# A fused Mamba, attention and mixture-of-experts kernel: the in-projection on 128 rows of taps, and one transfer of B and C for each chunk

## The chip, the cores and the metric

The kernel runs on one core of a Trainium2 chip, as one launch. The metric is the device time of the launch in microseconds (us); the time before is 5182.59 us, the median of three runs (5178.62 to 5191.08). The engines are called as in the profile: PE is TensorE's matmuls and PEld its weight loads, DVE is VectorE, ACT is ScalarE, POOL is GpSimd, and SP is SyncE, which here issues nearly all DMA transfers.

## The reference, cut to what matters

There are two layers on four images of 128 channels and 64x64 points (4096 tokens). The first normalises, runs a depthwise 3x3 convolution and a Mamba block, and projects; the second is attention with four heads over 4096 tokens and a mixture of eight experts. The change lies in the Mamba block. It cuts the 128 channels into four chunks of 32 that share their weights:

```python
xz = u @ in_proj_w.T                       # u: tokens x 32, in_proj_w: 128 x 32
xin, z = jnp.split(xz, 2, axis=-1)         # 64 channels each
xin = jnp.pad(xin, ((0, 0), (0, 0), (3, 0)))
xin = lax.conv_general_dilated(xin, conv1d_w[:, None, :], (1,), 'VALID', feature_group_count=di)
xin = silu(xin + conv1d_b[None, :, None])  # a causal convolution of four taps for each channel
x_dbl = xin @ x_proj_w.T
dt, Bm, Cm = jnp.split(x_dbl, [R, R + N], axis=-1)     # N = 16 states, R = 2
delta = softplus(dt @ dt_proj_w.T + dt_proj_b)
h = exp(delta * A) * h + delta * Bm * xin              # for each token, channel and state
y = einsum('bdn,bn->bd', h, Cm)
out = (y + D_skip * xin) * silu(z) @ out_proj_w.T
```

The in-projection of the first half and the convolution are both linear, so they can be one matmul: every output is a sum over 32 channels and 4 taps, 128 products in all.

## The kernel before

**Tiling.** The tokens of an image are cut into eight blocks of 512, so there are 32 blocks (b, i). Two chunks fill the 128 partitions (64 channels of each), so each block has two passes, p = 0 and 1. A pass has sixteen states, taken two at a time: a unit (b, i, p, n). There are 512 units.

**Slots.** The main loop runs over slots, two to a unit, so 1024 slots and 32 to a block; after them the loop goes on until the rest of the attention is done. Every engine works in the order in which its instructions are written. One slot writes, in this order:

1. transfers put off by `send` (they go out at the next slot's `flush`), then `fetch`: the rows of B or C of a later unit, one DMA on SP;
2. `prepared`: on ACT the decay exp(delta A) of the next unit (`da`), 128x512;
3. in even slots `driven` on DVE (h = B times du);
4. the X lane's second half-stage;
5. one group of attention: four matmuls of scores (`sc`) on PE and two exponentials of 128x1024 on ACT (`pT`);
6. in even slots `scan` on DVE, in odd slots `read` on DVE (C times h);
7. the Y lane's first half-stage;
8. `turned_on`: PE adds up and turns the terms of y;
9. the Y lane's second half-stage;
10. `weighted`: eight matmuls of the weighted sums (`av`) of the group of the slot before;
11. the X lane's first half-stage.

The scores have two PSUM buffers, so the scores of a slot wait until the exponentials of the slot before have been read out of them.

**Lanes.** Everything else runs as generators in two lanes, one stage for each half-slot (a `yield` ends a stage). A lane takes its tasks in order, and a task starts only when what it depends on is done. The Y lane holds `first_norm` (10 stages, 5 slots), `conv` (26 stages, 13 slots) and `inputs` (6 stages, 3 slots) of every block, and `group_norm` for every image. The X lane holds `closed` (18 stages, 9 slots; out-projection, projection, keys, queries and values of a block) and, from slot 2 of a block, `finished` (30 stages, 15 slots; a block's attention output and experts). Each lane has one PSUM bank, `work("X")` and `work("Y")`.

For block k the loop at L1311 appends to the Y lane: `inputs(k, 1)`, which waits for the scan of (k-1, 1); `first_norm` of block k+2; `conv` of k+1; `inputs(k+1, 0)`, which waits for the scan of (k, 0). `fetch` forces an `inputs` that isn't done by the time a unit's rows are wanted.

**The in-projection.** `conv` ends with `xn`, the normalised block with three tokens of the block before ahead of it. Four transfers of 64 partitions make `pairs`: rows 0 to 63 the two chunks of a pass, rows 64 to 127 the same one token later. `inputs` multiplies it in two accumulating matmuls (L667), a 128x128 weight for the taps 0 and 1 and one for 2 and 3. In its first stage it issues these and the matmul of z; in the second, one half-slot on, ACT's Silu of `xin` and of `zs`; in the third the matmuls `pb` (B and C) and `wdt`; in the fourth ACT's copy of B and C and the softplus in five pieces; in the sixth five DVE operations. A channel d of chunk c sits on partition 2d + c. `fetched` (L714) is one transfer of a row of B or C for both chunks to 128 partitions, 512 KB.

Of the kernel before, what the change touches and what calls it, by code (L numbers as in the profile page):

```python
# [17 lines left out]
P = 128  # L18
# [5 lines left out]
DI = 64  # L24
# [12 lines left out]
def conv_mamba_attn_moe_kernel(ctx: ExitStack, tc: tile.TileContext, t: dict):  # L37
# [37 lines left out]

    late = nc.scalar
    gmat, fc1w = (load(k, eng=late) for k in ("gmat", "fc1w"))
    inx, xdt, dtT, alog = (load(k, pool=scratch, eng=late) for k in ("inx", "xdt", "dtT", "alog"))
    cw = load("cw", [P, 4, P], t["cw"].partition_broadcast(P), pool=scratch, eng=late)
    lnw, lnb, fc1b, lcw, lcb = (load(k, eng=late) for k in ("lnw", "lnb", "fc1b", "lcw", "lcb"))  # L80
    fc2T, fc2b, cb, dtb, dsk = (load(k, eng=late) for k in ("fc2T", "fc2b", "cb", "dtb", "dsk"))
    inz, wbc, wout, projT = (load(k, eng=late) for k in ("inz", "wbc", "wout", "projT"))
# [10 lines left out]
        nc.vector.tensor_scalar_mul(taps[:, k, :], ident, fc1w[:, k : k + 1])  # L93


    inxc = const.tile([P, 2, P], F32, name="inxc")
    for j in range(4):
        r = slice(DI * (j % 2), DI * (j % 2) + DI)
        nc.vector.tensor_mul(inxc[r, j // 2, :], inx[r, :], cw[r, j, :])

    amat = const.tile([P, NST], F32, name="amat")
    nc.scalar.activation(amat, alog, AF.Exp)
# [319 lines left out]
    def send(out, in_, slots=1):  # L422
        outgoing.append([slots, out, in_])
# [24 lines left out]
    def work(lane, shape=None):  # L448
        return ps_work.tile(shape or [P, BLK], F32, tag=f"work{lane}", name=f"ps_{lane}")
# [51 lines left out]


    held = set()
    group_of, y0_of, xn_of, pairs_of, in_of, gated, kqv = {}, {}, {}, {}, {}, {}, {}
    IMAGE = "p (r w) -> p r w"
    group_of[0] = gm0, gr0

# [75 lines left out]
    def conv(b, i):  # L583
        cm = tmp("Y", "cm")
        h = work("Y") if b == 0 else cm
        half = b == i == 0

        def tap(k):
            y0 = y0_rows(b, i, k // 3, k % 3)
            w = fc1w[:, k : k + 1]  # L590

            hr = (cm if half and k > 4 else h).rearrange(IMAGE, w=IMG)
            if b == 0 and not (half and k > 4):
                mm(hr, taps[:, k, :], y0, k == 0, k == (4 if half else 8))
            elif k == 0 or half and k == 5:
                vector.tensor_scalar(hr, y0, w, fc1b, ALU.mult, ALU.add)
            else:
                vector.scalar_tensor_tensor(hr, y0, w, hr, ALU.mult, ALU.add)

        for k in range(0, 5 if half else 9, 2):  # L600
            if b:
                yield
            tap(k)
            if k < (4 if half else 8):
                tap(k + 1)
            if half and k < 4:
                tap(k + 5)
                tap(k + 6)
            if b == 0:
                yield  # L610
                if half and k == 4:
                    vector.tensor_add(cm, h, cm)
                elif k == 8:
                    scalar.activation(cm, h, AF.Identity, bias=fc1b)
            yield
        ps = transposed("Y", by_tile(cm))
        yield
        xt = yield from normalised("Y", by_tile(ps))
        ps = transposed("Y", xt)
        yield  # L620
        g = tmp("Y", "g")
        scalar.activation(g, ps, AF.Gelu, bias=lcb, scale=lcw)
        yield
        ps = work("Y")
        mm(ps, fc2T, g)
        yield
        cm = tmp("Y", "cm")
        vector.scalar_tensor_tensor(
            cm.rearrange(IMAGE, w=IMG), ps.rearrange(IMAGE, w=IMG), fc2b, y0_rows(b, i),
            ALU.add, ALU.add,  # L630
        )
        yield
        ps = transposed("Y", by_tile(cm))
        yield
        xt = yield from normalised("Y", by_tile(ps))
        ps = transposed("Y", xt)
        yield

        xn = mix.tile([P, 3 + BLK], F32, name="xn", bufs=3)
        scalar.activation(xn[:, 3:], ps, AF.Identity, bias=lnb, scale=lnw)  # L640
        if i == 0:
            gpsimd.memset(xn[:, 0:3], 0.0)
        else:
            gpsimd.tensor_copy(xn[:, 0:3], xn_of[b, i - 1][:, BLK : BLK + 3])
        xn_of[b, i] = xn

        pairs = mix.tile([P, 2, 2 + BLK], F32, name="pairs")
        for p in range(2):
            for late in range(2):
                send(  # L650
                    pairs[DI * late : DI * late + DI, p, :],
                    xn[DI * p : DI * p + DI, late : late + 2 + BLK],
                )
        pairs_of[b, i] = pairs
        yield
        yield
        yield

    def inputs(b, i, p):

        xn, pairs = xn_of[b, i], pairs_of[b, i]
        while held:
            yield
            yield
        held.add("in")
        ps = work("Y")
        summed(ps, [(inxc[:, j, :], pairs[:, p, 2 * j : 2 * j + BLK]) for j in range(2)])  # L667
        pz = work("X")
        mm(pz, inz[:, p, :], xn[:, 3:])
        yield  # L670
        xin = mix.tile([P, BLK], F32, name="xin", bufs=2)
        scalar.activation(xin, ps, AF.Silu, bias=cb)
        zs = mix.tile([P, BLK], F32, name="zs", bufs=4)
        scalar.activation(zs, pz, AF.Silu)
        yield

        pb = work("X")
        mm(pb, wbc, xin)
        ps = work("Y")
        mm(ps, wdt, xin)  # L680
        yield
        held.clear()
        bc = tmp("Y", "bc")[0:DI, :]
        scalar.copy(bc, pb[0:DI, :])
        bcd = dram.tile([2, NST // 2, 2, 2 * BLK], F32, name="bcd", bufs=4)
        send(bcd.rearrange("c n k (m q) -> (c n k m) q", m=2), bc)

        e = tmp("Y", "e")
        scalar.activation(e, ps, AF.Abs, bias=dtb)
        scalar.activation(e, e, AF.Exp, scale=-1.0)  # L690
        ln = tmp("Y", "ln")
        scalar.activation(ln, e, AF.Ln, bias=1.0)
        delta = mix.tile([P, BLK], F32, name="delta", bufs=2)
        scalar.activation(delta, ps, AF.Relu, bias=dtb)
        yield
        yield

        du = mix.tile([P, BLK], F32, name="du", bufs=2)
        lost = du
        vector.tensor_scalar(lost, e, 1.0, -1.0, ALU.add, ALU.add)  # L700
        vector.tensor_sub(lost, e, lost)
        vector.tensor_add(ln, ln, lost)
        vector.tensor_add(delta, delta, ln)
        vector.tensor_mul(du, delta, xin)
        in_of[b, i, p] = xin, zs, delta, du, bcd
        done.add(("in", b, i, p))
        yield
# [6 lines left out]
    def fetched(unit, k):  # L714

        b, i, p, n = unit
        w = mix.tile([P, 2, BLK], F32, name="rows", bufs=4)
        sync.dma_start(
            out=w.rearrange("p m q -> p (m q)"),
            in_=in_of[b, i, p][4][:, n // 2, k, :][None].to_broadcast([DI, 2, 2 * BLK]),  # L720
        )
        return w

    def decayed(unit, da, k):
# [584 lines left out]

    X.append((("y0", *blocks[1]), first_norm(*blocks[1], "X"), [("y0", *blocks[0])]))  # L1310
    for k in range(-2, len(blocks)):  # L1311
        if 0 <= k:
            b, i = blocks[k]
            Y.append((("in", b, i, 1), inputs(b, i, 1), [("scan", *blocks[k - 1], 1)] if k else []))
        if k + 2 < len(blocks):
            b, i = blocks[k + 2]
            if k + 2 == 0 or i > 0:
                upper(k + 2)
        if 0 <= k + 1 < len(blocks):
            b, i = blocks[k + 1]  # L1320
            below = [("y0", b, i + 1)] if i < NB - 1 else []
            Y.append((("xn", b, i), conv(b, i), before(k + 1, 3) + below))
            Y.append((
                ("in", b, i, 0), inputs(b, i, 0),
                before(k + 1, 2) + ([("scan", *blocks[k], 0)] if k >= 0 else []),
            ))

        if 0 < k + 2 < len(blocks) and blocks[k + 2][1] == 0:
            upper(k + 2)
# [113 lines left out]
def _laid_out(i):  # L1443
# [10 lines left out]


    def twice(a):
        return np.repeat(a, 2, axis=0)

    z = np.zeros((P, P), np.float32)
    inx, inz = z.copy(), np.zeros((P, 2, P), np.float32)  # L1460
    wout = np.zeros((P, 2, P), np.float32)
    wbc = np.zeros((P, 4, NST // 2, 2, 2), np.float32)
    xdt, dtT = np.zeros((4, P), np.float32), np.zeros((4, P), np.float32)
    for c in range(2):
        d = slice(c, P, 2)
        for p in range(2):
            s = slice(64 * p + 32 * c, 64 * p + 32 * c + 32)
            inx[s, d] = c0["in_proj_w"][:DI].T
            inz[s, p, d] = c0["in_proj_w"][DI:].T
            wout[d, p, s] = c0["out_proj_w"].T  # L1470

        wbc[d, c] = c0["x_proj_w"][2:].reshape(2, NST // 2, 2, DI).transpose(3, 1, 0, 2)
        xdt[2 * c : 2 * c + 2, d] = c0["x_proj_w"][:2]
        dtT[2 * c : 2 * c + 2, d] = c0["dt_proj_w"].T
# [5 lines left out]
    for h in range(NH):  # L1480
# [12 lines left out]
        "lcw": col(c0["lc_ln_w"]), "lcb": col(c0["lc_ln_b"]),  # L1493
        "fc1w": c0["lc_fc1_w"].reshape(C, 9), "fc1b": col(c0["lc_fc1_b"]),
        "fc2T": c0["lc_fc2_w"].T, "fc2b": col(c0["lc_fc2_b"]),
        "inx": inx, "inz": inz,
        "cw": twice(c0["conv1d_w"]).T,
        "cb": col(twice(c0["conv1d_b"])),
        "xdt": xdt, "dtT": dtT, "dtb": col(twice(c0["dt_proj_b"])),
        "wbc": wbc.reshape(P, -1), "alog": twice(c0["A_log"]),  # L1500
# [28 lines left out]
```

## Time and profile before

| | |
|---|---|
| median of three runs | 5182.59 us (5178.62 to 5191.08) |
| profiled execution, its own time | 5183.13 us |
| its span | 5180.9 us |
| mean granted TensorE clock | 0.957 |
| start, 0 to 130 us | PE busy 62.55 us |
| first image, 130 to 650 us | PE busy 356.25 of 520 us, DVE 424.94 us, clock 0.79 |
| 2600 to 3250 us | PE busy 621.57 of 650 us, DVE 535.46 us, ACT 517.93 us, clock 0.99 |
| after the last unit, 4570 to 5181 us | PE busy 567.52 of 611 us, DVE 171.89 us, ACT 303.99 us |
| matmuls of the in-projection | first at 62.0 us, last at 4459.1 us, 64 groups of four instructions |
| transfers issued | rows of B and C 1024, `pairs` 128, keys 320, values 320, queries 161 |

Busy time of an engine is the time in which at least one of its instructions runs; idle time is told with what ended it. A float32 matmul stands in the trace as two instructions. The table by stretches shows that the slots fall into three parts: a start and a first image in which attention has little to do yet, a long middle, and a tail that is attention and experts alone.

### The profile page before, as it was taken

The numbers are of one execution on the slowest core, as the hardware profiler recorded it, in microseconds if no ns is written. First come the engines' busy times: TensorE is split into PE (matmuls) and PEld (weight loads), VectorE is DVE, ScalarE is ACT, GpSimd is POOL, SyncE is SP. The second block draws the span as 40 slices with busy tenths as digits, with TensorE's granted clock in tenths as the row PEclk, the third lists the DMA queues.
The fourth block names the chain that finished last, engine by engine and source line by source line (L and its number), as shares of the span: only waits on it lengthen the run. The fifth ranks groups of instructions, "written<-read, shape, count | busy, mean of one in ns | idle before, by whom it ended". The sixth has DMA issues, their size and how long they took to land.

```text
span 5180.9 us, 62597 instructions
## 1 busy us (share of the span) xinstructions
PE 4710.1 (91%) x20684; PEld 2321.9 (45%) x20684; DVE 3835.8 (74%) x5780; ACT 3745.7 (72%) x5700; POOL 423.1 (8%) x483
## 2 busy tenths in 40 slices
PE   4567898999999998899999999999999999999997
PEld 2334444444444444444444444444444444443443
DVE  6987767877778887878788887888788877751332
ACT  4556777787787787688888787788777787656543
POOL 1111111100000000101000000000000001000000
PEclk7778999999999999899999999999999999999998
DMA  3556667677666766767766766777766666754542
GB/s 127 183 186 212 205 212 253 233 239 243 229 224 225 239 227 234 242 230 258 252 228 227 238 229 231 258 231 255 265 227 233 221 230 221 262 179 156 184 134 72
DMA packets 451693, 1131.70 MB, mean 218 GB/s; under 512 B 51858, under 2 KB 135331, under 8 KB 451363
## 3 DMA queue, kind: packets, MB, share of 16 engines
q1 hardware_dynamic: 447296, 1125.96, 64.3%
q8 instruction: 166, 2.72, 0.2%
q10 hardware_dynamic: 4066, 1.67, 0.1%
q14 instruction: 165, 1.34, 0.1%
HBM read 967.22 MB, written 143.39 MB: 214 GB/s over the span
## 4 chain that ended last, share of the span: by engine, by line
PE 59%; DVE 19%; ACT 10%; DMA 6%; issue 4%; POOL 2%; SPq 1%; DVEq 0%; ACTq 0%; POOLq 0%
PE av L406 25%; PE sc L406 14%; PE ps_X L406 9%; DVE h L406 6%; PE ps_Y L406 6%; PE y L406 5%; ACT pT L406 3%; ACT L406 2%; DVE hc L406 2%; DMA ks<-kd 2%; ACT xt L406 1%; DVE stX L406 1%; DVE du L406 1%; DMA rows<-bcd 1%; DVE cm L406 1%
## 5 line engine op out<-in xcount | busy, mean ns | idle before, releaser
L406 ACT ACTIVATE pT<-sc 128x1024 f32<-128x1024 f32 x2048 | 1984.3, 1022 | 934.3 <-PE sc L406 932.8
L406 PE MATMUL av<-pT,v 128*64 128x512 f32 x8192 | 2002.8, 610 | 10.8 <-DVE avs L406 10.8
L406 PE MATMUL sc<-qs,ks 128*128 128x512 f32 x4096 | 1302.7, 437 | 75.9 <-ACT pT L406 39.4
L406 DVE TENSOR_TENSOR_SCAN h<-da,state,h 128x1025 f32<-128x1025 f32 x512 | 1204.5, 2353 | 96.6 <-ACT h L406 62.8
L406 PEld LDWEIGHTS sc<-qs,ks 128*128 128x128 f32 x4096 | 703.1, 190 | 812.7 <-ACT pT L406 273.2
L406 PEld LDWEIGHTS av<-pT,v 128*64 128x64 f32 x8192 | 500.4, 137 | 845.7 <-issue 816.7
L406 ACT ACTIVATE da<-delta,amat 128x512 f32<-128x512 f32 x1024 | 742.9, 730 | 1.9
L406 PE MATMUL y<-ident,hc 128*128 128x128 f32 x4096 | 626.2, 284 | 64.6 <-DVE hc L406 64.6
L406 DVE TENSOR_TENSOR hc<-rows,h 128x1024 f32<-128x1024 f32 x512 | 624.6, 1220 | 15.3 <-PE y L406 5.4
L406 DVE TENSOR_TENSOR h<-rows,du 128x1024 f32<-128x1024 f32 x512 | 623.9, 1218 | 13.0 <-DMA rows<-bcd 8.5
L406 PEld LDWEIGHTS y<-ident,hc 128*128 128x128 f32 x4096 | 524.2, 147 | 229.0 <-issue 80.8
L406 ACT ACT_TABLE_LOAD x319 | 409.3, 1283 | 19.5 <-DVE zs L406 14.3
L406 POOL TENSOR_TENSOR rsX<-rsX,mhalf 128x4 f32<-128x4 f32 x92 | 203.7, 2214 | 2504.4 <-DVE rsX L406 2420.4
L406 POOL TENSOR_TENSOR rsY<-rsY,mhalf 128x4 f32<-128x4 f32 x100 | 130.7, 1307 | 2072.5 <-DVE shiftY L406 1561.5
L406 DVE TENSOR_TENSOR avs<-av,prev 128x512 f32<-128x512 f32 x96 | 66.2, 689 | 256.7 <-PE av L406 235.0
L406 PE MATMUL ps_X<-share,w_ew 128*128 128x512 f32 x432 | 213.9, 617 | 9.1 <-DVE share L406 8.8
L406 ACT ACTIVATE xt<-ps_Y,shiftY,rsY 128x128 f32<-128x128 f32 x380 | 143.6, 468 | 81.7 <-POOL shiftY L406 73.8
L406 DVE TENSOR_TENSOR share<-share,xf 128x1024 f32<-128x1024 f32 x128 | 156.0, 1219 | 16.5 <-DMA share<-sharesX 11.7
L406 ACT COPY state<-h 128x2 f32<-128x2 f32 x448 | 88.8, 198 | 92.0 <-DVE h L406 92.0
L406 DVE SCALAR_TENSOR_TENSOR cm<-y,w_fc1w,cm 128x512 f32<-128x512 f32 x195 | 145.1, 744 | 8.0 <-ACT y L406 4.5
L406 PE MATMUL ps_Y<-pairs,inxc 128*128 128x512 f32 x256 | 132.6, 643 | 15.5 <-DMA pairs<-xn 9.9
L406 PEld LDWEIGHTS ps_X<-share,w_ew 128*128 128x128 f32 x432 | 73.2, 189 | 147.0 <-issue 97.1
(248 smaller groups left out, 3437.2 us busy)
## 6 DMA issues: line engine op xcount, KB each, us to landing
rows<-bcd SPq DMA_DIRECT2D x1024, 512.0 KB
ks<-kd SPq DMA_DIRECT2D x192, 512.0 KB
qs<-qd SPq DMA_DIRECT2D x161, 512.0 KB
share<-sharesX SPq DMA_DIRECT2D x108, 512.0 KB
v<-vd SPq DMA_DIRECT2D x192, 256.0 KB
ks<-kd SPq DMA_DIRECT2D x128, 256.0 KB
avd<-avs SPq DMA_DIRECT2D x96, 256.0 KB
prev<-avd SPq DMA_DIRECT2D x96, 256.0 KB
```

What stands on the lines that cost most here:

```text
L406: return lambda *args, **kw: queued(op(*args, **kw))
```

## The change

The taps of one chunk, 32 channels times 4, now fill the 128 rows of a tile `fours`, so that one matmul of 128 rows and 64 columns makes the 64 channels of a chunk; two of them, for the two chunks, write partitions 0 to 63 and 64 to 127 of one PSUM bank. The transfers of `fours` come in two pairs: for p = 0 at the end of `conv`, for p = 1 in the fourth stage of `inputs(k, 0)`. `inputs` has eight stages (four slots) in place of six: an empty one, the in-projection just ahead of the weighted sums, then Silu of `xin` and the matmul of z, then Silu of `zs`, and the rest as before. A channel d of chunk c now sits on partition 64c + d, and `fetched` is two transfers of 64 partitions, one for each chunk. In the loop that fills the Y lane, `first_norm` of block k+2 comes ahead of `inputs(k, 1)`.

```diff
-    inx, xdt, dtT, alog = (load(k, pool=scratch, eng=late) for k in ("inx", "xdt", "dtT", "alog"))
-    cw = load("cw", [P, 4, P], t["cw"].partition_broadcast(P), pool=scratch, eng=late)
+    inx, cw, xdt, dtT, alog = (
+        load(k, pool=scratch, eng=late) for k in ("inx", "cw", "xdt", "dtT", "alog")
+    )
...
-    inxc = const.tile([P, 2, P], F32, name="inxc")
-    for j in range(4):
-        r = slice(DI * (j % 2), DI * (j % 2) + DI)
-        nc.vector.tensor_mul(inxc[r, j // 2, :], inx[r, :], cw[r, j, :])
+    inxc = const.tile([P, DI], F32, name="inxc")
+    nc.vector.tensor_mul(inxc, inx, cw)
...
-        pairs = mix.tile([P, 2, 2 + BLK], F32, name="pairs")
-        for p in range(2):
-            for late in range(2):
-                send(
-                    pairs[DI * late : DI * late + DI, p, :],
-                    xn[DI * p : DI * p + DI, late : late + 2 + BLK],
-                )
-        pairs_of[b, i] = pairs
-        yield
-        yield
-        yield
+        windows(b, i, 0)
+        yield
+        yield
+        yield
+
+    def windows(b, i, p):
+        fours = mix.tile([P, 2, BLK], F32, name="fours")
+        for c in range(2):
+            r = slice(DI * p + DI // 2 * c, DI * p + DI // 2 * (c + 1))
+            src = xn_of[b, i][r, :]
+            src = bass.AP(src.tensor, src.offset, (src.ap[0], (1, 4), (1, BLK)))
+            send(fours[:, c, :], src)
+        fours_of[b, i, p] = fours
 
     def inputs(b, i, p):
 
-        xn, pairs = xn_of[b, i], pairs_of[b, i]
+        xn, fours = xn_of[b, i], fours_of.pop((b, i, p))
         while held:
             yield
             yield
         held.add("in")
+        yield
         ps = work("Y")
-        summed(ps, [(inxc[:, j, :], pairs[:, p, 2 * j : 2 * j + BLK]) for j in range(2)])
+        for c in range(2):
+            mm(ps[DI * c : DI * c + DI, :], inxc, fours[:, c, :])
+        yield
+        xin = mix.tile([P, BLK], F32, name="xin", bufs=2)
+        scalar.activation(xin, ps, AF.Silu, bias=cb)
         pz = work("X")
         mm(pz, inz[:, p, :], xn[:, 3:])
         yield
-        xin = mix.tile([P, BLK], F32, name="xin", bufs=2)
-        scalar.activation(xin, ps, AF.Silu, bias=cb)
         zs = mix.tile([P, BLK], F32, name="zs", bufs=4)
         scalar.activation(zs, pz, AF.Silu)
+        if p == 0:
+            windows(b, i, 1)
         yield
...
-        sync.dma_start(
-            out=w.rearrange("p m q -> p (m q)"),
-            in_=in_of[b, i, p][4][:, n // 2, k, :][None].to_broadcast([DI, 2, 2 * BLK]),
-        )
+        for c in range(2):
+            sync.dma_start(
+                out=w[DI * c : DI * c + DI].rearrange("p m q -> p (m q)"),
+                in_=in_of[b, i, p][4][c, n // 2, k, :][None].to_broadcast([DI, 2 * BLK]),
+            )
...
     for k in range(-2, len(blocks)):
-        if 0 <= k:
-            b, i = blocks[k]
-            Y.append((("in", b, i, 1), inputs(b, i, 1), [("scan", *blocks[k - 1], 1)] if k else []))
         if k + 2 < len(blocks):
             b, i = blocks[k + 2]
             if k + 2 == 0 or i > 0:
                 upper(k + 2)
+        if 0 <= k:
+            b, i = blocks[k]
+            Y.append((("in", b, i, 1), inputs(b, i, 1), [("scan", *blocks[k - 1], 1)] if k else []))
...
-        d = slice(c, P, 2)
+        d = slice(DI * c, DI * c + DI)
```

The weights are laid out to match on the host, the same numbers in another order.

More of the change, by code (lines that the diff above doesn't have):

```diff
@@ L503, in conv_mamba_attn_moe_kernel @@
     held = set()
-    group_of, y0_of, xn_of, pairs_of, in_of, gated, kqv = {}, {}, {}, {}, {}, {}, {}
+    group_of, y0_of, xn_of, fours_of, in_of, gated, kqv = {}, {}, {}, {}, {}, {}, {}
     IMAGE = "p (r w) -> p r w"
@@ L1456, in twice @@
     def twice(a):
-        return np.repeat(a, 2, axis=0)
-    z = np.zeros((P, P), np.float32)
-    inx, inz = z.copy(), np.zeros((P, 2, P), np.float32)
+        return np.concatenate([a, a])
+    inz = np.zeros((P, 2, P), np.float32)
     wout = np.zeros((P, 2, P), np.float32)
@@ L1464, in _laid_out @@
     for c in range(2):
-        d = slice(c, P, 2)
+        d = slice(DI * c, DI * c + DI)
         for p in range(2):
             s = slice(64 * p + 32 * c, 64 * p + 32 * c + 32)
-            inx[s, d] = c0["in_proj_w"][:DI].T
             inz[s, p, d] = c0["in_proj_w"][DI:].T
@@ L1495, in _laid_out @@
         "fc2T": c0["lc_fc2_w"].T, "fc2b": col(c0["lc_fc2_b"]),
-        "inx": inx, "inz": inz,
-        "cw": twice(c0["conv1d_w"]).T,
+        "inx": np.repeat(c0["in_proj_w"][:DI].T, 4, axis=0), "inz": inz,
+        "cw": np.tile(c0["conv1d_w"].T, (DI // 2, 1)),
         "cb": col(twice(c0["conv1d_b"])),
```

## The prediction

> **What bounds the kernel now.** I read the busy times first, then the groups with shapes kept apart, the waits of PE and of SP's queue, and last the timeline around a pass's in-projection. From the page and the groups:
>
> ```profile
> PE 4710.1 (91%) x20684; PEld 2321.9 (45%) x20684; DVE 3835.8 (74%) x5780; ACT 3745.7 (72%) x5700; POOL 423.1 (8%) x483
> L406 PE MATMUL ps_Y<-pairs,inxc 128*128 128x512 f32 x256 | 132.6, 643 | 15.5 <-DMA pairs<-xn 9.9 <-ACT delta L406 5.6
> L406 PE MATMUL ps_X<-zs,w_wout 128*64 128x512 f32 x128 | 33.1, 595 | 0.0
> L406 ACT ACT_TABLE_LOAD x319 | 409.3, 1283 | 19.5 <-DVE zs L406 14.3
> ```
>
> PE is busy 91% of the span, so taking matmul time away looks like a sure gain. The second and third lines give its size: four instructions of the in-projection are one pass, four of the out-projection the same kind of pair that the change makes (two matmuls of 64 columns on two halves of the array), at half the busy time. But an average hides where PE isn't the limit. The timeline of one pass (p = 0 of block 12; start, duration, engine, operation):
>
> ```profile
> 1630.52 1.88 PE L406 MATMUL ps_Y<-pairs,inxc 128*128 128x512 f32 x4
> 1632.23 1.02 PE L406 MATMUL ps_X<-xn,w_inz 128*128 128x512 f32 x2
> 1632.26 1.28 ACT L406 ACT_TABLE_LOAD   x1
> 1633.56 0.69 ACT L406 ACTIVATE xin<-ps_Y,w_cb 128x512 f32<-128x512 f32 x1
> 1634.74 1.28 ACT L406 ACT_TABLE_LOAD   x1
> 1635.49 1.12 PE L406 MATMUL ps_X<-xa,w_wqn 128*128 128x512 f32 x2
> 1639.20 1.02 PE L406 MATMUL ps_Y<-xin,wdt 128*128 128x512 f32 x2
> 1641.63 1.28 ACT L406 ACT_TABLE_LOAD   x1
> 1644.23 1.28 ACT L406 ACT_TABLE_LOAD   x1
> 1647.21 0.73 PE L406 MATMUL sc<-qs,ks 128*128 128x512 f32 x2 [0.35 <-ACT pT L406]
> 1648.12 0.73 PE L406 MATMUL sc<-qs,ks 128*128 128x512 f32 x2 [0.18 <-ACT pT L406]
> 1651.92 1.02 ACT L406 ACTIVATE pT<-sc 128x1024 f32<-128x1024 f32 x1 [0.62 <-PE sc L406]
> ```
>
> ACT loads its table four times in one pass and is busy nearly all the time from 1630 to 1650 us; at 1647 PE already waits for it. Only after that does ACT wait for PE again. So a pass is a place where ACT is as late as PE, and what PE saves there may only lengthen its wait. SP's queue and the transfers that PE waits for:
>
> ```profile
> SPq L406 <- DVE hc L406: 1199.2, 301, 9.8
> PE sc L406 <- DMA ks<-kd: 35.4, 16, 5.1
> L406 SPq DMA_DIRECT2D rows<-bcd x1024: 512/519/2047, 71.4 to 4563.1; - x171
> ```
>
> SP spends much of its time waiting for a buffer of rows to come free, not issuing, and PE has waited for keys only 16 times.
>
> [...] The trace has the 1283 ns, but the next activation starts 1.30 us after the load (1632.26 to 1633.56), so I charge 1.29 us. [...]
>
> **The change part by part.** Sums are made against the profiled execution, 5183.1 us, 0.5 above the median.
>
> *Matmuls.* Eight instructions of the weighted sums start-to-start take 1.87 us, so four take 0.94; the old in-projection takes 1.72 start to start (1630.52 to 1632.23), 1.88 alone. PE's work falls by 0.78 to 0.94 us a pass; 64 passes, 50 to 60 us. That is the whole gain that there can be, nearly.
>
> *The fourth slot.* I follow both queues slot by slot through a block, with start-to-start times of the trace. An ordinary slot is 3.43 us of PE (scores 1.03, y 0.53, weighted sums 1.87) and 2.56 us of ACT (decay and copies 0.74, exponentials 1.82). Before, a pass adds to its first slot 2.58 us of PE (in-projection 1.72, z 0.86) and 3.92 of ACT (two loads, two Silus, 0.14 to empty), to its second 1.72 of PE (`pb`, `wdt`) and 5.6 of ACT (copy 0.46, 0.72, 0.65, load 1.29, 0.54, 0.67, load 1.29). After, the first slot has 0.94 of PE and nothing for ACT, which waits there as in any ordinary slot; the second 0.86 of PE and 3.92 of ACT; the third 1.72 and 5.6. So PE's work no longer lies beside ACT's, and the saving comes out of slots in which PE waits for ACT anyway. [...]
>
> *Where the slots come to lie.* Slots of a block count from 0. Before: `inputs` of p = 1 in 3 to 5 (its scan is done at 3), `first_norm` 6 to 10, `conv` 11 to 23, `inputs` of p = 0 in 24 to 26. After: p = 1 in 3 to 6, `conv` 7 to 19, p = 0 in 20 to 23, `first_norm` 24 to 28. The X lane doesn't move: `finished` 2 to 16, `closed` 17 to 26, whose normalisation on ACT (four activations, 1.6 us of it beyond cover) falls in slot 22. In the trace 11 slots lie between p = 0 and p = 1, and 21 back, as counted.
>
> For p = 0 slots 21 to 23 then hold PE 4.29 + 5.70 + 4.37 = 14.4 us (with `closed`'s 0.55 and 0.94) and ACT 6.5 + 9.8 + 3.1 = 19.4. ACT may be about 1 us late without harm, so PE stands 4 to 4.6 us, in slot 24. Before, slots 24 to 26 held PE 6.95 + 6.25 + 3.43 = 16.6 and ACT 6.5 + 8.2 + 2.6 = 17.3, and PE stood 0.73 (seen: 0.35 and 0.18). For p = 1 slots 3 to 8 sum to 28.7 us before and 28.6 after. Over a whole block the recurrence gives 142.6 us before (the trace has 145.7 as the mean of fourteen blocks from 2216 to 4256 us; DVE and DMA waits are left out of mine) with 1.4 us of PE standing, and 146.1 after with 6.5. So +3.5 us a block: 5.1 more standing, 1.6 less work.
>
> By blocks: 17 blocks with `closed` just there (11 to 30 but 15, 18, 23), 60 us. The three ends of an image (15, 23, 31), where `inputs` of p = 0 was at 19 and meets the same normalisation now, 3.3 each, 10. Blocks 4 to 10 and 18, where nothing of X lies beside p = 0: a bare pass gives +1.0, 8 us. The first four blocks are in DVE's part of the run; half of their 0.9 to 1.9 us a pass, and 2 us at the start, come back: 8 us gained.
>
> *DVE.* The nine taps of `conv` (0.74 us each) move from slots 11 to 15 to 7 to 11, beside the routing of `finished` in slot 9 (about 3 us of small operations) and behind the five operations of `du` (3 us, slot 6). By sums DVE ends 3.6 us late at slot 12, where PE wants the result; before, 0.9 us late at 16. At most 2.6 us in 20 blocks, 52 us; at least nothing, since PE's wait in slot 7 helps DVE, and a gain of 10 if the empty slots that `first_norm` now fills even things out. I take 10.
>
> *SP.* 1024 more issues of 0.52 us: 532 us on a queue that issues about 1500 in all. Queued behind each are keys, values and queries, wanted three slots later. The rows themselves are wanted three slots after. The 16 waits for keys grow by 0.52 each: 8 at most if nothing else waits; I take 5. `fours` doubles `pairs`' bytes (16 MB of 1132 MB), has half a slot more to land and issues as often; nothing. The matmul of z no longer has the in-projection ahead to cover the X lane's reading of the same bank: within the 5.
>
> Sum: 60 + 10 + 8 + 10 + 5 - 8 = +85; 5183 + 85 = 5268 us.
>
> **The rivals.** *PE decides everywhere* (faster, the other side): middle stretches are 95% PE (621.57 of 650 us), X's matmuls fill ACT's late slots, and the standing of PE doesn't grow. Then 64 times 0.94, less the half of ten early ones and 4 us for transfers: -52, 5131. It decides once X's matmuls beside a pass reach about 1.4 us a slot, or if `closed` lies two slots earlier than counted. Against it: the 0.35 and 0.18 us waits, and ACT without a gap. *No change*: the p = 0 loss is half as large and cancels the saving, 5183. *SP is late*: two issues in each slot delay keys or rows, every one of 320 key loads by 0.52 us where a quarter is felt, and more after waits for `hc`: 5225. Against it: 1199 us of waiting that would shrink first. *The halves don't run side by side*: the pair costs 1.88 again: 64 x 0.94 = 60 on top, 5328; the out-projection speaks against it.
>
> **How the numbers follow.** Chances: ACT's lag 0.52, PE everywhere 0.32, no change 0.06, SP 0.06, not side by side 0.04. This measurement can tell 0.3%, 15.5 us, from none. So faster 0.32, same 0.06, slower 0.62. The likeliest case's own range: 5205 (p = 0 loses half) to 5325 (DVE's 52 in full). To hold eight in ten it must reach into the faster case: 5125 to 5320.
>
> **What would show it.** Right: in-projection about 0.95 us a pass beside the weighted sums, 15 slots from p = 0 to p = 1 and 17 back, and PE waiting 3 to 5 us for `pT` two to four slots after the in-projection of p = 0, with PE's total wait for `pT` up by 60 us or more from 39.4. Wrong: those waits unchanged with 50 us less PE time and a shorter middle; a wait for keys or rows well over 35 us; or waits for `cm` growing from 3.6 us past 40, which would put DVE in ACT's place.

## The result, and the profile after

The changed kernel takes 5330.24 us, the median of six runs (5317.9 to 5343.06). The kernel before took 5186.3 us in the six runs beside it. The ratio is 1.0279, with a 95% interval of 1.0259 to 1.0299: slower by 144 us. The sign is the forecast's. The size isn't: 5330 lies above the forecast of 5268 and above the upper end of its range.

First the page of the changed kernel, from its parts on busy time, queues, the chain that ended last and groups:

```profile
PE 4713.2 (88%) x20684; PEld 2311.0 (43%) x20684; DVE 3843.3 (72%) x5777; ACT 3746.4 (70%) x5700; POOL 454.6 (9%) x483
...
q1 hardware_dynamic: 471872, 1142.74, 78.1%
...
PE 44%; DMA 18%; DVE 17%; ACT 13%; issue 5%; SPq 1%; POOL 1%; DVEq 0%; ACTq 0%; POOLq 0%
...
L405 DVE TENSOR_TENSOR h<-rows,du 128x1024 f32<-128x1024 f32 x512 | 623.4, 1218 | 48.9 <-DMA rows<-bcd 48.8
```

The same two parts of the kernel before, for queues and chain:

```profile
q1 hardware_dynamic: 447296, 1125.96, 64.3%
...
PE 59%; DVE 19%; ACT 10%; DMA 6%; issue 4%; POOL 2%; SPq 1%; DVEq 0%; ACTq 0%; POOLq 0%
```

A queue's columns are packets, megabytes, and the time that its packets took as a share of 16 engines' span. The bytes grew by 1.5%, the share from 64.3% to 78.1%. In the chain, DMA's part tripled, from 6% to 18%, and PE's fell from 59% to 44%. That is not the picture that was forecast, in which ACT takes PE's place; ACT grew by 3 points only. The last line of the first fence says where DVE met it: 48.8 us of waiting for rows of B and C, against 8.5 before.

PE does its part of the change. The group of the in-projection, shapes kept apart:

```profile
L405 PE MATMUL ps_Y<-fours,inxc 128*64 128x512 f32 x256 | 84.0, 650 | 8.8 <-DMA fours<-xn 8.5
```

It was 132.6 us. Yet PE's sum stayed (4710.1 to 4713.2), since the other matmuls, the same in number, grew, among them the weighted sums from 2002.8 to 2017.3 us and the scores from 1302.7 to 1307.1. The mean granted clock fell from 0.957 to 0.948.

What PE waits for in the changed kernel (total us, times, longest):

```profile
PE ps_Y L405 <- ACT xt L405: 122.5, 31, 8.0
PE sc L405 <- DMA ks<-kd: 71.0, 32, 6.6
PE sc L405 <- ACT pT L405: 50.3, 71, 3.5
...
PE ps_X L405 <- ACT xa L405: 45.9, 18, 5.3
```

Two of them in the kernel before, to compare:

```profile
PE ps_Y L406 <- ACT xt L406: 69.1, 21, 7.7
PE sc L406 <- ACT pT L406: 39.4, 117, 2.2
```

Two things grew. Waits ended by ACT, all lines added up, went from 148 to 274 us, most of the growth under `xt` and `xa` (0.3 before). Under `xt`, a step of the normalisations, ACT is for the most part not behind with its own work: it waits there for POOL itself, 163.2 us now and 73.8 before. Waits for keys doubled, from 35.4 to 71.0. And SP's queue, in its own view of waits:

```profile
SPq L405 <- DVE hc L405: 734.7, 255, 10.2
...
SPq L405 <- DMA rows<-bcd: 239.0, 413, 1.7
```

The wait for `hc` shrank from 1199.2, as expected of a queue with 1024 more issues. The second line is new in size: 239.0 us where SP waited for an earlier transfer of rows, 24.2 before. So it isn't only issuing that holds up the queue; transfers that are still under way do too.

### The profile page after: what moved, and what is told of

It is laid out like the page before. It is cut to its first block, busy times and chain, and to the rows that moved or that the text cites. A ratio compares the mean times of both kernels' runs of the same rounds, so it can differ in the third digit from the quotient of the medians.

```text
span 5331.4 us, 64105 instructions
## 1 busy us (share of the span) xinstructions
PE 4713.2 (88%) x20684; PEld 2311.0 (43%) x20684; DVE 3843.3 (72%) x5777; ACT 3746.4 (70%) x5700; POOL 454.6 (9%) x483
## 3 DMA queue, kind: packets, MB, share of 16 engines
q1 hardware_dynamic: 471872, 1142.74, 78.1%
## 4 chain that ended last, share of the span: by engine, by line
PE 44%; DMA 18%; DVE 17%; ACT 13%; issue 5%; SPq 1%; POOL 1%; DVEq 0%; ACTq 0%; POOLq 0%
PE av L405 19%; PE sc L405 11%; DVE h L405 7%; PE ps_X L405 7%; ACT pT L405 5%; PE ps_Y L405 4%; DMA rows<-bcd 4%; DMA ks<-kd 4%; PE y L405 4%; ACT L405 3%; DVE hc L405 2%; DVE cm L405 2%; SPq L405 1%; ACT xt L405 1%; DMA v<-vd 1%
## 5 line engine op out<-in xcount | busy, mean ns | idle before, releaser
L405 PE MATMUL av<-pT,v 128*64 128x512 f32 x8192 | 2017.3, 612 | 10.7 <-DVE avs L405 9.8
L405 PE MATMUL sc<-qs,ks 128*128 128x512 f32 x4096 | 1307.1, 440 | 123.4 <-DMA ks<-kd 71.0
L405 PEld LDWEIGHTS av<-pT,v 128*64 128x64 f32 x8192 | 511.7, 138 | 850.1 <-issue 815.3
L405 DVE TENSOR_TENSOR h<-rows,du 128x1024 f32<-128x1024 f32 x512 | 623.4, 1218 | 48.9 <-DMA rows<-bcd 48.8
L405 POOL TENSOR_TENSOR rsY<-rsY,mhalf 128x4 f32<-128x4 f32 x100 | 162.9, 1629 | 2883.5 <-DVE shiftY L405 2344.9
L405 ACT ACTIVATE xt<-ps_Y,shiftY,rsY 128x128 f32<-128x128 f32 x380 | 143.7, 465 | 170.7 <-POOL shiftY L405 163.2
L405 PE MATMUL ps_Y<-ident,xt 128*128 128x128 f32 x380 | 68.5, 309 | 123.1 <-ACT xt L405 122.5
L405 DVE TENSOR_TENSOR res<-res,ps_X 128x512 f32<-128x512 f32 x108 | 74.1, 686 | 96.2 <-PE ps_X L405 95.3
```

What stands on the lines that cost most here:

```text
L405: return lambda *args, **kw: queued(op(*args, **kw))
```

## The experiments

A kernel named "before with ..." starts from the kernel before, one named "changed with ..." from the changed kernel. The kernel before ran beside them on the same chip; its medians there were 5182 to 5187 us, and each gain or loss is the difference to the one beside it.

**Which part costs the 144 us.** First the transfers alone: the kernel before, with its rows fetched in two transfers of 64 partitions each.

```diff
+        for c in range(2):
             sync.dma_start(
-                out=w.rearrange("p m q -> p (m q)"),
-                in_=...[:, n // 2, k, :][None].to_broadcast([DI, 2, 2 * BLK]),
+                out=w[DI * c : DI * c + DI].rearrange("p m q -> p (m q)"),
+                in_=...[:, n // 2, k, :][None].to_broadcast([DI // 2, 2, 2 * BLK]),
             )
```

> The kernel before with one edit: each row transfer of B and C is cut into two, partitions 0 to 63 and 64 to 127, same bytes. Theory R (the cut into two neighbouring halves makes the transfers slower, and rows, keys and values land late): most of the loss, 80 to 140 us slower, busy share of the DMA queue from 64% to about 78%, PE waits for keys over 60 us. Theory S (the four-slot in-projection and its place cost the time): within 20 us of before. Theory I (only the number of issues on SP counts): as R in time, but the DMA share rises by no more than 2 points.

5290.44 us, ratio 1.0202 [1.0185, 1.0219]: +103 us with no matmul and no slot changed. To see whether it is the number of issues, the same two issues with the same bytes, but to the even and to the odd partitions:

```diff
+                out=w[c::2].rearrange("p m q -> p (m q)"),
+                in_=...[c, n // 2, k, :][None].to_broadcast([DI, 2 * BLK]),
```

> The kernel before with each row transfer cut into two by chunk, the even and the odd partitions: as many issues as the halves, but each transfer spread over all 128 partitions. Theory R: within 25 us of before, DMA share 64 to 67%. Theory I: as slow as the halves, 60 us or more over before. Theory S: within 20 us of before.

5190.61 us, ratio 1.0008 [1.0001, 1.0016]: +3 us. The queue of the halves, and PE's wait for keys:

```profile
q1 hardware_dynamic: 463680, 1126.03, 77.9%
...
PE sc L406 <- DMA ks<-kd: 87.0, 38, 7.3
```

The same with even and odd partitions:

```profile
q1 hardware_dynamic: 463680, 1126.03, 65.1%
...
PE sc L406 <- DMA ks<-kd: 37.9, 19, 5.7
```

Packets and megabytes are equal to the last digit, and so is the number of issues (2048). What differs is which partitions one transfer writes, and with it the engines' busy share (13 points), the wait for keys and 100 us. The side that is read differs too: a half here reads the rows of both chunks, the even or the odd partitions read one. But each half of the changed kernel also reads one row, and its queue stands at 78.1%, so it isn't that. The 1024 added issues, taken by themselves, are worth 3 us. In PE's own account of the halves' 103 us, 69 are more waiting for DMA, 12 for DVE, 4 less for ACT, and 25 are PE busy longer. By windows, from 2600 to 3250 us (busy us and instructions of PE, PEld, DVE, ACT, POOL; then clock, DMA share, GB/s), first the halves and then even and odd:

```profile
2600.00:3250.00 650.00, 617.77 (x2786) 307.98 (x2782) 525.37 (x792) 512.19 (x791) 50.89 (x60) 0.98 0.83 226
```

```profile
2600.00:3250.00 650.00, 627.06 (x2832) 309.44 (x2829) 535.79 (x799) 519.55 (x803) 53.16 (x60) 0.99 0.69 232
```

In the same time the halves get 46 fewer matmuls done, with the engines 83% busy instead of 69% at a lower rate.

Then the rest of the change. The changed kernel with the one row transfer of before (what each half of the channels gets is told in the expectation):

```diff
-        for c in range(2):
-            sync.dma_start(out=w[DI * c : DI * c + DI]..., in_=...[c, n // 2, k, :]...)
+        sync.dma_start(out=w..., in_=...[:, n // 2, k, :][None].to_broadcast([DI, 2, 2 * BLK]))
```

> The changed kernel with the one row transfer of before put back as it was; it lays the rows of B and C on the partitions of the old channel order, so the scan reads the other chunk's rows for half of its channels. Theory R+S (row transfers and slots each cost, nearly additive): 5220 to 5250 us, DMA share 65%, PE waits for keys under 45 us. Theory R alone: 5130 to 5180 us. Theory S alone: 5300 us or more.

5215.61 us, ratio 1.0056 [1.0039, 1.0073]: +32, a little below the 5220 to 5250 that were expected of two costs that add up. So in the changed kernel the split rows cost 144 - 32 = 112 us, and all the rest 32. Its DMA engines are busy 65.7%, PE's wait for keys was 22.9 us, and waits ended by ACT summed to 280 us, near the changed kernel's 274. ACT's lag comes with the slots, the wait for keys with the rows.

The changed kernel with the six stages and the order of before, and the same once more with the single row transfer:

```diff
-        yield
         ps = work("Y")
         ...
-        yield
-        xin = ...; scalar.activation(xin, ps, AF.Silu, bias=cb)
         pz = work("X")
         mm(pz, inz[:, p, :], xn[:, 3:])
         yield
+        xin = ...; scalar.activation(xin, ps, AF.Silu, bias=cb)
```

> The changed kernel with the old six stages (in-projection, then z, in the first half-slot, both Silus in the second) and the old order of the Y lane; the 64-column matmuls, the four-tap transfers and the two row transfers stay. Theory S: 5130 to 5190 us. Theory R: 5240 to 5320 us, DMA share 78% still.

> The changed kernel with the old stages, the old lane order and the one row transfer of before (rows of B and C on the partitions of the old channel order, as above): the 64-column matmuls and four-tap transfers alone. If PE decides in a pass: 5125 to 5150 us. If ACT holds PE in a pass anyway or the four-tap transfers land late: 5170 to 5210 us, with PE waits for fours of 10 us or more.

The first: 5313.24 us, 1.025 [1.0228, 1.0272], +126. The second: 5186.47 us, 1.0003 [0.9994, 1.0011], +2. What is left in the second are the matmuls on two halves of the array and the four-tap transfers. Its in-projection is 97.5 us of PE against 132.6, and the time doesn't move. This is the second case of its expectation: PE waits 12.3 us for `fours`. Two of its passes, the first with p = 0 and the second with p = 1:

```profile
1636.62 1.89 PE L405 MATMUL ps_Y<-fours,inxc 128*64 128x512 f32 x4
1680.31 1.08 PE L405 MATMUL ps_Y<-fours,inxc 128*64 128x512 f32 x4
```

In 28 of the 32 passes with p = 0 the second half starts over 0.3 us after the first, in none with p = 1: in the old slots the in-projection comes right behind the transfers, the second lands late (PE's weight loads wait for `fours` 31 times), and the halves no longer run side by side. With single rows and the new slots it is 5 of 32. From the start of the in-projection to the start of the matmul behind it, the 64 passes take 94.5 us against 122.0, so this run has about half of the saving that was forecast. Even that doesn't show: PE's busy time falls by 8 us in all, and its waits grow by 12, those for keys from 35.4 to 47.4 and for `pT` from 39.4 to 47.6.

The new slots with the old matmuls and transfers:

> The kernel before with the new stages of inputs (eight in place of six) and the new order of the Y lane, but the old matmuls and transfers. Theory S: 100 us or more slower, 15 slots from p = 0 to p = 1, PE waits for xt and xa as in the changed kernel. Theory R: at most 60 us slower (the recurrence of the prediction gives it the 85 us, less what DVE and SP were charged, plus nothing saved in matmuls), DMA share 64%.

5252.28 us, 1.0129 [1.011, 1.0149]: +65, a little over the 60 of theory R, with the waits for `xt`, `xa` and `pT` of the changed kernel (123.2, 47.3 and 48.2 us). Set against the +32 with the new matmuls, these save 33 us once they stand beside the weighted sums. They have a gain, then, but only in slots that cost twice as much.

**Why the slots cost.** Each half of the move alone: eight stages in the old order, and the old stages with `first_norm` put ahead of `inputs` of p = 1.

> The kernel before with the eight stages of inputs alone, old lane order, matmuls and transfers. The recurrence of the prediction gives a full block 4.5 us more for this and 5.1 with the new order, so theory ACT (the stage parts PE's work from ACT's): 45 to 75 us slower, nearly all of the 65 us of the new slots. Theory place (what counts is that p = 0 moves beside the normalisation of closed): within 20 us of before.

> The kernel before with first_norm of block k+2 ahead of inputs(k, 1) in the Y lane and nothing else. Theory ACT: within 15 us of before (the recurrence gives 0.2 us a block). Theory place: 40 to 65 us slower, since p = 0 starts at slot 19 now.

Stages alone: 5255.28 us, 1.0133 [1.0116, 1.015], +71. Order alone: 5238.98 us, 1.0109 [1.0092, 1.0126], +55. Together they cost 65, so they don't add. Their waits differ in kind. PE's waits with the stages alone:

```profile
PE sc L406 <- ACT pT L406: 92.6, 93, 3.5
```

PE's waits with the order alone:

```profile
PE ps_X L406 <- DVE bothX L406: 75.3, 25, 4.1
```

They are 39.4 and 45.5 us in the kernel before: ACT is late in the one, DVE in the other. With the order alone `xt` grew too, from 69.1 to 100.1 us, but 91.4 of it lie before block 8 (counted from 0), which starts only 1 us later than before; by block 30 the run is 50 us behind. To test that ACT's lag is made of its table loads, Identity took the place of Silu and Ln in `inputs` (which leaves those functions out), so that a pass loads no table. An activation takes as long either way (687 and 688 ns for `xin`), and the 64 loads that are left, of 319, belong to other operations.

```diff
-        scalar.activation(xin, ps, AF.Silu, bias=cb)
+        scalar.activation(xin, ps, AF.Identity, bias=cb)
```

> The kernel before with Identity in place of Silu and Ln in inputs, so that a pass of the in-projection loads no activation table; the base of the next two. About 256 of 319 table loads go, 330 us of ACT's time. Theory ACT (ACT holds PE in a pass): 20 to 60 us faster than before. Otherwise within 15 us of before.

> The eight stages of inputs with Identity in place of Silu and Ln. Theory ACT: the 71 us that the stages cost shrink to less than 25 against the same kernel with six stages. If something else in the stages costs (DVE, the longer lane): 50 us or more stay.

> The new order of the Y lane with Identity in place of Silu and Ln. If the 55 us of the order are ACT's (p = 0 beside the normalisation of closed): less than 20 stay. If they are DVE's (the taps of conv beside the routing of finished): 35 us or more stay against the same kernel in the old order, and the waits of PE and ACT for the routing stay up.

Without loads the kernel before takes 5150.52 us, 0.9937 [0.9921, 0.9954]. The eight stages then take 5115.53 us, 35 less than that: what cost 71 us now gains. The order takes 5202.59 us, 52 more than without it, nearly the 55 from before. The two waits from above, with the stages and with the order, both without loads:

```profile
PE sc L406 <- ACT pT L406: 7.4, 32, 0.6
```

```profile
PE ps_X L406 <- DVE bothX L406: 73.6, 25, 4.1
```

So the stages' cost is ACT's table loads, and the order's is not. That the order's is DVE's is what the waits point to; no run changed DVE's work there.

A dose between: Silu by way of Tanh, with three operations more for DVE in each pass. This has two loads in a pass instead of four.

```diff
-        scalar.activation(xin, ps, AF.Silu, bias=cb)
+        scalar.activation(th, ps, AF.Tanh, bias=cbh, scale=0.5)
+        vector.tensor_scalar(th, th, 1.0, 0.5, ALU.add, ALU.mult)
+        vector.scalar_tensor_tensor(xin, ps, cb, th, ALU.add, ALU.mult)
```

> The kernel before with Silu in inputs made from Tanh, which needs no other table than Exp if the compiler puts it there, and three DVE operations on 128x512 for each pass; Ln stays, so about 128 of 319 table loads go. If ACT's loads hold PE in a pass: 0 to 25 us faster than before, less what DVE gives back. If DVE is in the way: slower.

> The same in the eight stages, old lane order. With half of the loads gone the stages' cost of 71 us should fall to about half or less against the run before; between the 35 us gain without any load and 30 us of loss.

The page of the first has the loads:

```profile
L408 ACT ACT_TABLE_LOAD x192 | 246.3, 1283 | 3.4
```

There were 319 before, so the 128 activations with Tanh (687 ns for the one of `xin`, as with Silu) have no load of their own. By itself it changes nothing: 5188.34 us, 1.0009 [0.9999, 1.0018]; PE's waits ended by ACT fell by 26 us, and those ended by DVE, which has more to do now, rose by 36. With the eight stages, 5204.62 us, 1.0041 [1.0028, 1.0053], which is 16 more than without them. So the stages cost 71, 16 and -35 us with four, two and no loads in a pass; the middle one has DVE's added work in it.

**Why the halves cost.** Three transfers each, of 64, 32 and 32 partitions, so with the same number of issues and the same sizes. In the first the large one is a half (0 to 63), in the second it is the middle (32 to 95):

```diff
+        for lo, hi in ((0, 64), (64, 96), (96, 128)):
+        for lo, hi in ((32, 96), (0, 32), (96, 128)):
```

> The kernel before with each row transfer cut into three, partitions 0 to 63, 64 to 95 and 96 to 127. Every transfer lies in the lower or in the upper half. If the half decides: DMA share 77% or more and 90 us or more over before. If the count of transfers or of issues decides, the same as the next run.

> As the run beside it, but the three are partitions 32 to 95, 0 to 31 and 96 to 127: as many issues and the same sizes, with the large one across both halves and the two small ones, in opposite halves, one after the other. If the half decides: DMA share 66 to 72% and at most 50 us over before. If it is that a transfer writes neighbouring partitions at all: as slow as the thirds.

Thirds: 5304.34 us, 1.0218 [1.0195, 1.0241], +121. Middle: 5247.31 us, 1.0117 [1.01, 1.0133], +64. Their queues, the thirds' first:

```profile
q1 hardware_dynamic: 480064, 1126.09, 76.2%
```

```profile
q1 hardware_dynamic: 480064, 1126.09, 69.0%
```

With the large transfer across the middle it is 57 us and 7 points less than with one that fills a half; its two small ones also lie in opposite halves, which wasn't separated from that. By time the layouts come out as even-and-odd (+3 us, the queue's share 65.1%), the middle (+64, 69.0%), halves (+103, 77.9%) and thirds (+121, 76.2%). Between halves and even-and-odd the busy time of all 16 engines differs by 0.779 x 5283.7 - 0.651 x 5194.6 = 734 us. Why the engines take longer with a transfer that fills a half, no run shows. The middle's +64 is more than the 50 that were expected at most. It is 53% of the thirds' 121, and half of its bytes still go out in small transfers that lie in one half each.

**A remedy that failed.** If what hurts is a transfer into half the partitions, one transfer into all 128 should mend it. In the changed kernel with the old stages and order, each row of B and C was stored eight times, so that one transfer could fetch both chunks' rows in sixteen pieces of eight partitions.

> The changed kernel with the old stages and lane order, and eight copies of every row of B and C written to DRAM, so that one transfer with a source of sixteen rows, each read eight times, fills all 128 partitions. Theory R (a transfer that writes only one half of the partitions is what is slow): 5190 to 5220 us, that is most of the 127 us that the two transfers cost here come back, though 63 MB more are written; DMA share 66 to 71%. If only the count of issues mattered, the same time; if the source (one row read 64 times) made it slow, no less than 5260 us, as each row is still read 64 times.

5333.06 us, 1.0288 [1.0271, 1.0305], against 5313.24 with the two halves: 20 us worse. Its queue:

```profile
q1 hardware_dynamic: 487232, 1201.41, 81.6%
```

This writes all partitions, and the engines are busier still, with 59 MB more to move and another pattern on the side that is read. Set against the run with single rows and the old slots (65.8% for 1142.67 MB), the engines' time grew by 0.816 x 5330.5 - 0.658 x 5184.8 = 938 us. An estimate: at that run's 3.0 us a MB, 59 MB would take 175 us. So the bytes look like the smaller part, but the pattern wasn't tested alone.

None of the kernels that compute everything is better than the kernel before; the closest are even-and-odd at +3 and Tanh at +5.

## Why the prediction was right, and where it wasn't

**The step that failed** is the term of SP and its transfers: "1024 more issues of 0.52 us ... I take 5". The issues were sized well, 3 us by the even-and-odd run, though the queue issued 2932 transfers before and not about 1500. What the term didn't price is how long each half occupies the engines (the 734 us between halves and even-and-odd). It counted issues and never asked which partitions a transfer reaches. In place of the 5 us this measured 112 us in the changed kernel and 103 in the kernel before. So this term alone was 107 us short; that the whole sum was only 59 short (+85 for +144) is luck, since the rest was 48 us too high. The prediction's own marker ("a wait for keys or rows well over 35 us") came out at 71.0 and 48.8 us. The rival "SP is late" had the right victims and another cause: keys and rows late, 42 us, through a queue of issues. What it held against itself, the long wait for `hc`, did shrink first, to 734.7 us.

**ACT's lag**, the likeliest case, is right in its mechanism and too large: the sum without SP's term said +80, and the run with single rows measured +32. The slots lie as counted, 15 from p = 0 to p = 1 and 17 back. The in-projection takes 0.91 us start to start beside the weighted sums (0.94 forecast). One pass of p = 0 in the changed kernel, by timeline (start, duration, engine; in brackets the idle time before it):

```profile
2867.97 1.08 PE L405 MATMUL ps_Y<-fours,inxc 128*64 128x512 f32 x4
2868.88 1.89 PE L405 MATMUL av<-pT,v 128*64 128x512 f32 x8
...
2872.36 1.94 ACT L405 ACTIVATE pT<-sc 128x1024 f32<-128x1024 f32 x2 [3.37 <-PE sc L405]
...
2874.32 1.28 ACT L405 ACT_TABLE_LOAD   x1
...
2876.87 1.28 ACT L405 ACT_TABLE_LOAD   x1
...
2882.77 0.66 PE L405 MATMUL ps_X<-ident,xt 128*128 128x128 f32 x4 [1.04 <-ACT bc L405]
...
2889.14 1.13 PE L405 MATMUL ps_X<-xa,w_wkn 128*128 128x512 f32 x2 [2.48 <-ACT xa L405]
...
2890.98 0.73 PE L405 MATMUL sc<-qs,ks 128*128 128x512 f32 x2 [0.18 <-ACT pT L405]
```

ACT stands 3.37 us for want of work in the slot of the in-projection, then loads tables, and PE stands 1.04 + 2.48 + 0.18 = 3.7 us for it. The forecast had 4 to 4.6. But it stands under the names `bc` and `xa`, matmuls of the other lanes that come ahead of the scores in PE's order, so PE's wait for `pT` grew by 11 us and not by the 60 that the prediction offered as its sign. The sum over all names ended by ACT is the better sign, if it is taken stretch by stretch.

The start times of the scans, 16 to a block, allow that. With single rows block 4 starts at 522.5 us (531.5 before) and block 8 at 1074.1 (1076.7): the early blocks gain 9 us by block 4, where the forecast had 8, although PE's waits for `xt` before block 8 grow by 37 us. From block 8 to block 30 (4323.1, before 4288.2) the run loses 37 us, where the forecast's terms for these blocks come to 67 (16 x 3.5 + 2 x 3.3 + 4 x 1.0). In that stretch:

| PE, blocks 8 to 29 | forecast | measured |
|---|---|---|
| more standing for ACT | 102 us (16 x 5.1 + 2 x 4.9 + 4 x 2.6) | 95 us (34.3 to 129.0) |
| less busy time | 35 us (22 x 1.6) | 19.5 us |
| less waiting for DVE and DMA | no term | 39 us (121.4 to 82.1) |

The 4.9 and 2.6 are the forecast's 3.3 and 1.0 with 1.6 of saved work added. So the standing was sized well. PE's busy time falls by little over half of what was forecast, since its other matmuls took longer (the weighted sums 2012.8 us in the whole run, 2002.8 before). And the third line is missing: where PE is held up by ACT, it meets less waiting for others. That the one wait covers the other is the reading that fits; no run tested it alone.

**DVE**: the forecast took 10 of at most 52 us. The order alone costs 55, with DVE late (`bothX`) and with no part of ACT's loads in it, so the upper bound was the right size for that edit alone. (The range's upper end, 5325, doesn't follow from it: with 52 in place of 10 the sum is +127, 5310.) In the full slots the wait for `bothX` is 30.8 us, below the 45.5 of before. `cm`, named as DVE's marker, was at 9.9: DVE's lag showed under another name, and in the full slots it may be covered by ACT's.

**The matmuls**: two halves side by side take 1.08 us for what took 1.88, so that rival is out; its 5328 us lie beside the measured 5330 by chance. From the start of the in-projection to the start of the matmul behind it, the 64 passes took 122.0 us before and 68.3 with single rows, 54 saved, within the forecast 50 to 60. *PE decides everywhere* promised -52, and with that saving and single rows the kernel takes 32 us more. "Nothing" for the four-tap transfers is nearly right in the new slots (PE waits 8.5 us for `fours`, 9.9 for `pairs` before) and wrong in the old ones.

## What to carry to other kernels

Before a saving is priced, look at which engine is late in the slot that it leaves and in the slot that it goes to; and where several engines are late in turn, don't simply add their lags: here 95 us more waiting for one came with 39 less for the others. When a broadcast or load is cut in two, ask which partitions each part reaches: here every second one was nearly free (+3 us), two halves cost 2% (+103), and of three transfers, those with the large one across the middle cost half as much as those with it in one half (+64 against +121). Equal bytes and packets with a higher busy share of the DMA engines (77.9% against 65.1% here) are the sign.

## What the runs showed of the hardware that was not expected

- Two kernels with the same issues, packets and bytes differ by 100 us and by 77.9% against 65.1% of DMA engine time, through the partitions that each transfer writes.
- The granted clock isn't a constant of the chip between kernels. In the profiled executions it was 0.957 in the kernel before, 0.953 with the halves, 0.951 with the stages alone, 0.952 in the changed kernel with single rows, 0.948 in the changed kernel (0.944 to 0.951 over its six runs). With the halves PE is busy 4735.4 us for the same 20684 matmuls that took 4710.1. It isn't simply lower where the kernel is slower: with the new slots and old matmuls it was 0.956 at 5252 us. What sets it wasn't tested, so how much of each loss goes through the clock stays open; PE's 25 us more of busy time are a quarter of the halves' loss.
- The eight stages, a loss of 71 us in the kernel as it is, gain 35 us in one whose passes load no table; taking out half of the loads without moving the stages, at the price of three DVE operations a pass, brought nothing.
- A change between matmuls of 128 and of 64 columns cost about 0.1 us here, which the prediction's sum leaves out. The old in-projection takes 1.72 us start to start ahead of a matmul of 128 columns and 1.81 ahead of the weighted sums, with 64 (new slots, old matmuls); the new one 1.01 ahead of 128 columns (old slots) and 0.91 ahead of the weighted sums.
